# Attention over pairs 4 to 7 of a batch in one stretch instead of two

## The chip, the cores and the metric

The kernel runs on one core of a Trainium2 chip. The metric is the device time in microseconds; the kernel before takes 1127.67 us (median of three runs, 1126.29 to 1128.37). Work goes to TensorE (matrix products, from SBUF into the accumulators in PSUM), VectorE, ScalarE and GpSimd (elementwise work; the first two empty PSUM), and SyncE, whose queue issues DMAs. In a profile they are PE (PEld for its weight loads), DVE, ACT, POOL and SP.

## The reference

For x of shape (8, 512, 256), in float32, four blocks are added one after the other, each on a layer norm LN of x:

```python
# 1: linear attention       Q, K, V = n @ Wq.T, n @ Wk.T, n @ Wv.T      (n = LN(x))
x = x + l2norm(Q) * (sum over rows of l2norm(K) * V) / 512
# 2: gated feed-forward, p = LN(x) shifted down by one row
xr, xk = mu_r * n + (1 - mu_r) * p, mu_k * n + (1 - mu_k) * p
x = x + sigmoid(xr @ Wr.T) * (square(relu(xk @ Wk.T)) @ Wv2.T)
# 3: softmax attention, 16 heads of 64, with biases
x = x + concat(softmax(q k.T / 8, over the query axis) v) @ l_w.T + l_b
# 4: the same feed-forward as in 2, with the same weights
```

The softmax is over the query axis (axis 2 of the scores), so a key's row of scores holds its whole sum.

## The kernel before

Batches are processed as a pipeline. `linear`, `queries`, `mean`, `front`, `front_ffn` and `front_norm` (the "front") do blocks 1 and 2 and the norm of block 3 for a batch; each step that has to turn rows into columns goes through `normed_dma`: statistics on VectorE (L399, L400), a shift and a scale on GpSimd (L417 to L420), the normalisation on ScalarE (L423), a copy on GpSimd (L450), a transposing DMA on the SP queue (L455) and a copy on GpSimd (L459). For block 3 this leaves the tile `xta` (256 x 512, columns); `sums_of_rows` (L877) adds differences of its quarters, `xts`.

The 16 heads of a batch are eight pairs, p = 0 to 7; g = 8b + p numbers them over all batches. `project_pairs(g)` (L953) makes queries and keys of two pairs, g and g + 1, into two `qk` tiles, by a seven-product scheme for 2 x 2 blocks (`seven`, L898): seven products of TensorE, each of four matmuls with 256 columns (L968), and between them sums on VectorE and ScalarE (L920, L930, L940, L976, L984) on which later products depend. `values_fast` does the same for the values of four pairs (L1005), `project_out_fast` for the output (L1148), `keys` for one product of the last feed-forward (L623). The differences of weights and biases that the scheme needs are made at the start.

Attention of a pair is four steps c (128 keys of each head). `scores` (L1265) makes the scores of a step in eight matmuls on 64 x 64 quarters of the array (L1277), and VectorE takes their maxima (L1283); `exps` takes the exponentials on ScalarE with the sums beside (L1294); `scale_v` divides the values by the sums (VectorE L1307, GpSimd L1311); `context` (L1318) multiplies, again in eight quarter matmuls (L1331), and after the last step ScalarE and VectorE add the two halves (L1338, L1339). The context of a pair runs one pair or one step behind its scores.

Nothing is scheduled by the compiler: the program writes the instructions of every engine in the order that the class `Order` finds. It knows a modelled time for every step (`yield "V", 0.62, ready` is a step on VectorE of 0.62 us; T, A, G and S are TensorE, ScalarE, GpSimd and SyncE), keeps a modelled clock for each engine, and picks the step that can start first; `PLAN` gives each kind of step a due pair and a lead, and `CHOICES`, one entry for each window, shifts the window's share of TensorE time, the slack and the choice between steps. The main loop (L1400) goes over pairs by two: `attend(first)` is one stretch of attention for two pairs, in which other engines get steps only where `order.fill(0.0, 1.0)` finds them room; TensorE does nothing else there. Then comes a window of projections: `project_pairs` of the next two pairs is due in it, and front, values, output and last feed-forward (`tail`) of neighbouring batches fill it. So a batch has four stretches and four windows, behind pairs 1, 3, 5 and 7:

```python
    for first in range(0, G, 2):
        g = order.period = first + 1
        attend(first)
        if g + 1 < G:
            order.add(project_pairs(g + 1), "pairs", g)
        share = (total - order.spent) / ((G - first) // 2) + order.choice[0]
        order.until(g, share)
```

In the last batch the output is made plainly, in two halves (`project_out`), the first behind pair 5. The pool `heads` holds two `qk` tiles. Other things that the change touches: `vb` is the value bias, `dvb` the difference of its parts, `lb` the output bias, added to x by GpSimd in the last batch (L821); the squares for the norms of keys and queries go into a tile of their own, `sq` (L711, L742).

Of the kernel before, what the change touches and what calls it, by code (L numbers as in the profile page):

```python
# [8 lines left out]
F32 = mybir.dt.float32  # L9
U16 = mybir.dt.uint16  # L10
AF = mybir.ActivationFunctionType
ALU = mybir.AluOpType
# [18 lines left out]
PAIRS, BANKS = 3, 2  # L31
X_LANDS = (4.1, 8.5, 12.0)
# [7 lines left out]
    (0, 2, 3079, ((18, 1), (24, 1), (34, 1), (39, 2), (69, 1), (89, 1), (103, 1), (107, 1), (117, 1), (118, 1), (130, 1), (144, 1), (145, 1), (146, 1), (147, 2))),  # L40
    (0, 2, 24122, ((7, 3), (11, 1), (59, 1), (116, 2), (148, 1))),
    (-7, 1, 4847, ((5, 2), (8, 1), (13, 2), (15, 1), (24, 2), (25, 2))),
    (6, 0, 20556, ((24, 3),)), (3, -1, 86816, ((20, 1), (43, 1))),
    (4, 0, 84218, ((12, 1), (24, 2))), (-4, -1, 2976, ((40, 2),)), (0, 2, 77253, ((20, 1),)),
    (0, 2, 52854, ((34, 2),)), (6, 0, 62490, ((11, 3), (23, 1), (69, 2))),
    (-1, 0, 20876, ((7, 1),)), (-6, 0, 25653, ((58, 1),)), (-2, 1, 2103, ((72, 2),)),
    (-1, 0, 81629, ((7, 2), (8, 3), (67, 2))), (2, 0, 43246, ((52, 1),)),
    (0, 0, 79119, ((1, 2), (7, 1), (26, 2), (30, 2))), (6, -1, 2477, ()),
    (2, 0, 39734, ((33, 3),)),
    (-1, 1, 40203, ((14, 1), (31, 1), (32, 2), (38, 2), (55, 1), (60, 1))),  # L50
    (-1, 0, 0, ((1, 1), (20, 1), (25, 1), (37, 1))), (-2, 1, 35196, ((30, 1), (95, 2))),
    (-2, -1, 46703, ((16, 1), (66, 1))), (3, -1, 26797, ()),
    (-2, 2, 17874, ((9, 2), (10, 1), (20, 2))), (1, -1, 36974, ((2, 1), (7, 1))),
    (-2, 0, 3147, ((14, 3), (63, 1), (77, 3))),
    (4, 0, 77531, ((6, 2), (19, 2), (53, 3), (54, 1))), (-2, 2, 9675, ((18, 1), (42, 1))),
    (-1, 0, 83991, ((17, 2),)), (4, 2, 81239, ((31, 1),)), (-2, 2, 86574, ((24, 1),)),
    (-3, 0, 50919, ()), (0, -1, 4080, ()), (-2, 2, 82040, ((34, 1),)),
# [11 lines left out]
    "y rows": (4, 8), "y plain": (2, 0), "y last": (11, 16), "scale": (0, 128),  # L69
# [35 lines left out]
class Order:  # L105
# [5 lines left out]
    def __init__(self):  # L111
# [3 lines left out]
        self.last, self.asked = None, 0  # L115
# [101 lines left out]
    @property  # L217
    def choice(self):
        return CHOICES[min((self.period + 1) // 2, len(CHOICES) - 1)]
# [58 lines left out]
def kernel(ctx: ExitStack, tc: tile.TileContext, a: dict, out: bass.AP):  # L278
# [1065 lines left out]
    def attend(g):  # L1344

        for c in range(NT):
            if c == 3:
                order.at_once(scale_v(g, 0))
# [129 lines left out]
```

## Time and profile before

| | |
|---|---|
| median of three runs | 1127.67 us |
| the profiled execution | 1127.63 us, span 1125.9 us |
| stretches of attention | 32 of two pairs, 13.9 us each without waits (the first is cut in two) |
| windows of batch 2, behind pairs 1, 3, 5, 7 | 24.4, 16.6, 9.5, 31.2 us |
| other waits of TensorE | 6.2 us for the first normalised rows; 0.5 to 0.7 us at 44.7, 46.4 and 51.3 us |

The profile is of one execution. A window's or stretch's length is the time from its first matmul's start to the first start of what follows. Matmuls are pipelined and their ends are modelled, so lost time is read from starts. Engines other than TensorE cost time only where TensorE waits for them.

### The profile page before, as it was taken

The page shows a single profiled execution, that of the slowest core. Times are in us where ns is not written, and L with a number is a line of the kernel's source. Part 1 is how long each engine was busy: PE and PEld are TensorE (multiplying, and loading weights), DVE is VectorE, ACT ScalarE, POOL GpSimd, SP SyncE. Part 2 cuts the span into 40 slices and gives each one's busy share as a digit, 9 for nine tenths or more (in the row PEclk, how much of TensorE's full clock was granted, in tenths as well). Part 3 has the DMA queues.
Part 4 walks back from the last instruction along what each step waited for, and adds up shares of the span by engine and source line. Part 5 has one row for each costly group of instructions (what it writes and reads, how often), then busy time and mean ns, then how long its engine had stood idle before and what let it go on. Part 6 is the DMA issues. An engine that isn't in the chain of part 4 may idle for free. (4 is left out here: it accounts for less than half of the span.)

```text
span 1125.9 us, 19587 instructions
## 1 busy us (share of the span) xinstructions
PE 1107.2 (98%) x6938; PEld 699.6 (62%) x6938; DVE 801.4 (71%) x1743; ACT 677.2 (60%) x1779; POOL 589.1 (52%) x909
## 2 busy tenths in 40 slices
PE   7999999999999999999999999999999999999998
PEld 4655566665766657666567556676565764766556
DVE  5777677768676785777866777568786678666765
ACT  4666666468455774566745676447766377554653
POOL 4596346454465554654657456475454854344311
PEclk9999999999999999999999999999999999999999
DMA  8001001110112101111111211112100111001001
GB/s 302 11 10 30 10 2 20 20 29 10 20 38 39 29 10 29 34 34 20 21 29 47 20 29 20 42 24 29 26 20 23 29 29 21 1 20 29 19 1 38
DMA packets 83426, 34.18 MB, mean 30 GB/s; under 512 B 73088, under 2 KB 81920, under 8 KB 82816
## 3 DMA queue, kind: packets, MB, share of 16 engines
q1 hardware_dynamic: 82432, 31.87, 12.5%
q8 instruction: 55, 0.90, 0.3%
q10 hardware_dynamic: 864, 1.05, 0.3%
q14 instruction: 43, 0.35, 0.1%
q0 software_dynamic: 32, 0.00, 0.0%
HBM read 10.89 MB, written 4.19 MB: 13 GB/s over the span
## 5 line engine op out<-in xcount | busy, mean ns | idle before, releaser
L1294 ACT ACTIVATE e<-sc,nm 128x512 f32<-128x512 f32 x512 | 345.9, 690 | 113.4 <-DVE nm L1283 112.4
L1283 DVE TENSOR_REDUCE nm<-sc 128x1 f32<-128x512 f32 x512 | 322.6, 681 | 36.3 <-PE sc L1277 35.7
L1277 PE MATMUL sc<-qk 64*64 64x512 f32 x2048 | 267.1, 593 | 3.0 <-DVE qk L940 2.0
L1331 PE MATMUL cx<-e,vs 64*64 64x512 f32 x2048 | 264.8, 590 | 1.2 <-POOL vs L1311 1.2
L1311 POOL TENSOR_TENSOR vs<-v,rs 128x256 f32<-128x256 f32 x128 | 78.5, 615 | 261.5 <-DVE rs L1307 258.7
L1331 PEld LDWEIGHTS cx<-e,vs 64*64 64x64 f32 x2048 | 86.0, 133 | 136.1 <-issue 111.3
L1277 PEld LDWEIGHTS sc<-qk 64*64 64x64 f32 x2048 | 81.7, 133 | 133.7 <-issue 99.7
L1294 ACT ACTIVATION_READ_ACCUMULATOR e<-sc,nm 128x1 f32 x512 | 106.1, 207 | 0.0
L976 ACT ACTIVATE qk<-m_qk,bias 128x256 f32<-128x256 f32 x124 | 51.9, 472 | 51.8 <-PE m_qk L968 51.5
L1339 DVE TENSOR_TENSOR ctx<-cx,ctx 128x512 f32<-128x512 f32 x64 | 44.2, 691 | 41.2 <-ACT ctx L1338 40.8
L984 DVE SCALAR_TENSOR_TENSOR qk<-m_qk,dbias,qk 128x256 f32<-128x256 f32 x124 | 54.1, 478 | 22.4 <-PE m_qk L968 20.7
L1338 ACT COPY ctx<-cx 128x512 f32<-128x512 f32 x64 | 37.6, 587 | 38.3 <-PE cx L1331 38.0
L704 PE MATMUL kv<-wkv,xrFalse 128*128 128x512 f32 x112 | 54.0, 611 | 0.0
L459 POOL COPY xrFalse<-xkFalse 128x1024 uint16<-128x1024 uint16 x24 | 32.0, 1334 | 27.9 <-DMA xkFalse<-xrFalse 27.9
L450 POOL COPY xrFalse<-xnFalse 128x512 uint16<-128x512 uint16 x72 | 41.8, 613 | 6.2 <-ACT xnFalse L423 6.2
L1148 PE MATMUL m_y<-ctx,al 128*128 128x256 f32 x168 | 39.9, 381 | 0.0
L968 PE MATMUL m_qk<-xta,aq 128*128 128x256 f32 x124 | 39.0, 396 | 0.7 <-ACT qk L976 0.7
L968 PE MATMUL m_qk<-xta,sums_q 128*128 128x256 f32 x124 | 37.7, 385 | 0.0
L968 PE MATMUL m_qk<-xta,ak 128*128 128x256 f32 x124 | 36.9, 379 | 0.0
L968 PE MATMUL m_qk<-xts,ak 128*128 128x256 f32 x124 | 36.9, 379 | 0.0
L968 PE MATMUL m_qk<-xta,sums_k 128*128 128x256 f32 x124 | 36.9, 379 | 0.0
L968 PE MATMUL m_qk<-xts,aq 128*128 128x256 f32 x124 | 36.9, 379 | 0.0
(272 smaller groups left out, 2123.7 us busy)
## 6 DMA issues: line engine op xcount, KB each, us to landing
out<-x SPq DMA_DIRECT2D x16, 256.0 KB, 2.1
x<-in_x SPq DMA_DIRECT2D x6, 512.0 KB, 4.0
aq<-in_aq SPq DMA_DIRECT2D x1, 1024.0 KB, 8.4
ak<-in_ak SPq DMA_DIRECT2D x1, 1024.0 KB, 10.4
av<-in_av SPq DMA_DIRECT2D x1, 1024.0 KB, 12.4
al<-in_al SPq DMA_DIRECT2D x1, 1024.0 KB, 10.3
xkFalse<-xrFalse SPq DMA_TRANSPOSE x36, 3.1
x<-in_x SPq DMA_DIRECT2D x4, 128.0 KB, 3.6
```

Of the source, the lines that this page charges most:

```text
L450: nc.gpsimd.tensor_copy(apart.rearrange("p (l k u d) -> p l k u d", l=2, k=KC, u=2)[:, :, :, u, :], xn[:, u, :].rearrange("p (k d l) -> p ...
L704: nc.tensor.matmul(ps, lhsT=xt[:, kc, u * P : (u + 1) * P], rhs=wkv[:, kc, :], start=(kc == 0), stop=(kc == KC - 1),)
L968: nc.tensor.matmul(ps[:, w * HS : (w + 1) * HS], lhsT=lhs[w][n - 1], rhs=block_of_rows(b, n), start=start and w == 0, stop=True, skip_grou ...
L976: nc.scalar.activation(dst[:, w, :], ps[:, w, :], AF.Identity, bias=bias[:, w, p : p + 1])
L984: nc.vector.scalar_tensor_tensor(dst[:, w, :], ps[:, w, :], dbias[:, w, p // 2 : p // 2 + 1], part[:, w, :], ALU.add, ALU.add,)
L1148: nc.tensor.matmul(ps, lhsT=lhs[n - 1][:, g, :], rhs=rhs[g][n - 1], start=first and g == 0, stop=True, skip_group_check=True,)
L1277: nc.tensor.matmul(ps[j][m * HD : (m + 1) * HD, :], lhsT=kt[hs, keys], rhs=qt[hs, :], start=True, stop=True,)
L1283: nc.vector.tensor_reduce(nm[:, j : j + 1], ps[j], AX.X, ALU.max, negate=True)
L1294: nc.scalar.activation(e[:, j, :], ps[j], AF.Exp, bias=nm[:, j : j + 1], accum_out=sums[g, h][:, c % 2, j : j + 1],)
L1311: nc.gpsimd.tensor_tensor(vs, vh[b, p // 4][:, 2 * h : 2 * h + 2, cols].rearrange("p t (j d) -> p t j d", j=2), rs.unsqueeze(3).to_broadca ...
L1331: nc.tensor.matmul(cx[m][j * HD : (j + 1) * HD, :], lhsT=vsc[g, c // 2][ks, c % 2, j, :], rhs=es[g, c][ks, j, :], start=(c == 0), stop=(c ...
L1339: nc.vector.tensor_tensor(ct, cx[1], ct, ALU.add)
```

## The change

A batch now has three stretches, of pairs 0 and 1, 2 and 3, and 4 to 7, and three windows, behind pairs 1, 3 and 7. The window behind pair 3 has two `project_pairs`, for pairs 4/5 and 6/7, and the pool of `qk` tiles has four. A window's share of TensorE's time goes by the number of pairs in the stretch before it. `CHOICES` has a new list, one entry for the start and one for each of the 24 windows.

The room in SBUF for two more `qk` tiles comes from elsewhere: `sq` goes (the squares are written where the product, or the queries, are written afterwards); the tile `sums` is made for one of two buffer sets; `lb` goes, and its 256 numbers are loaded late in batch 6's output into a block of weight sums that is no longer used, from where GpSimd adds them in batch 7; `vb` keeps half of its numbers, and `dvb` holds the other half until the first plain values are made (two additions of 256 columns instead of one of 512), and only then becomes the difference. The first output half of batch 7 comes behind pair 7, since there is no window behind pair 5.

```diff
-    heads = ctx.enter_context(tc.tile_pool(name="heads", bufs=2))
+    heads = ctx.enter_context(tc.tile_pool(name="heads", bufs=4))
...
-    vb = const.tile([P, H * HD], F32, tag="vb", name="vb")
-    lb = const.tile([P, 1, D], F32, tag="lb", name="lb")
+    vb = const.tile([P, 2, 2 * P], F32, tag="vb", name="vb")
...
-    nc.sync.dma_start(out=vb, in_=a["vb"].partition_broadcast(P))
+    for half in range(2):
+        for dst, at in ((vb, 0), (dvb, 1)):
+            cols = slice((2 * half + at) * 2 * P, (2 * half + at + 1) * 2 * P)
+            nc.sync.dma_start(out=dst[:, half, :], in_=a["vb"][cols].partition_broadcast(P))
...
-    nc.sync.dma_start(out=lb[:, 0, :], in_=a["lb"].partition_broadcast(P))
...
-            sq = one.tile([P, D], F32, tag="sq", name=f"sqk_{b}_{h}_{u}")
-            nc.scalar.activation(sq, ps[:, :D], AF.Square, accum_out=ss[:, u : u + 1])
+            nc.scalar.activation(
+                kv[:, u, :], ps[:, :D], AF.Square, accum_out=ss[:, u : u + 1]
+            )
...
         if b == B - 1:
-            yield "G", 1.3, ready
-            xh = xb[:, 2 * h : 2 * h + 2, :]
-            nc.gpsimd.tensor_tensor(xh, xh, lb.to_broadcast([P, 2, D]), ALU.add)
+            order.add(biased(b, h, ready), "bias", NP * b)
+
+    def biased(b, h, ready):
+
+        yield "G", 1.3, ready, -1, "lb"
+        xh, lb = x[b][:, 2 * h : 2 * h + 2, :], blocks["sums_y"][:, 0:1, :D]
+        nc.gpsimd.tensor_tensor(xh, xh, lb.to_broadcast([P, 2, D]), ALU.add)
...
-            nc.vector.tensor_tensor(vh[b, half][:, t, :], ps, vb[:, cols], ALU.add)
+            for i, part in enumerate((vb, dvb)):
+                at = slice(i * 256, i * 256 + 256)
+                nc.vector.tensor_tensor(
+                    vh[b, half][:, t, at], ps[:, at], part[:, half, :], ALU.add
+                )
             order.give()
         order.marks[f"v_{b}_{half}"] = ready
+        yield "G", 1.3, ready
+        nc.gpsimd.tensor_tensor(dvb, dvb, vb, ALU.subtract)
+        order.marks["dvb"] = ready
...
+            nc.sync.dma_start(
+                out=blocks["sums_y"][:, 0, :D], in_=a["lb"].partition_broadcast(P)
+            )
+            order.marks["lb"] = p4 + 2.5
...
-    def attend(g):
...
+    def attend(first, n):
+
+        for g in range(first, first + n):
+            behind = 1 if g > first else 0
+            for c in range(NT):
+                if c == 3 and g < first + n - 1:
+                    order.at_once(scale_v(g, 0))
+                scores(g, c)
+                if c == 1 and g > first:
+                    order.at_once(scale_v(g - 1, 1))
+                if g > 0 and c >= behind:
+                    context(g - 1, c - behind)
+                elif g == 0:
+                    order.fill(BANK)
+                if behind and c == 3:
+                    context(g - 1, 3)
+                exps(g, c)
+                order.fill(0.0, 1.0)
...
-    halves_of = vb.rearrange("p (g i c) -> p g i c", i=2, c=2 * P)
-    nc.gpsimd.tensor_tensor(dvb, halves_of[:, :, 1, :], halves_of[:, :, 0, :], ALU.subtract)
...
-    for first in range(0, G, 2):
-        g = order.period = first + 1
+    lengths = {NP * b + 4: 4 for b in range(B)}
+    first = 0
+    while first < G:
+        n = lengths.get(first, 2)
+        g = order.period = first + n - 1
+        order.step += 1
...
-        if p == 5 and b == B - 1:
+        if p == 3 and b == B - 1:
             order.add(project_out(b, 0), "y plain", g)
...
-        if g + 1 < G:
-            order.add(project_pairs(g + 1), "pairs", g)
+        for i in range(1, lengths.get(g + 1, 2), 2):
+            if g + i < G:
+                order.add(project_pairs(g + i), "pairs", g)
...
-        share = (total - order.spent) / ((G - first) // 2) + order.choice[0]
+        share = (total - order.spent) * n / (G - first) + order.choice[0]
```

## The prediction

> **What bounds the kernel now.** I read the page's busy shares first, then TensorE's timeline around the places where it changes between attention and projections, then the eight windows behind pair 5 of each batch, and last VectorE's timeline at a late start of attention. The page, engine shares and granted clock:
>
> ```profile
> PE 1107.2 (98%) x6938; PEld 699.6 (62%) x6938; DVE 801.4 (71%) x1743; ACT 677.2 (60%) x1779; POOL 589.1 (52%) x909
> ...
> PEclk9999999999999999999999999999999999999999
> ```
>
> TensorE is the bound nearly everywhere, at its full clock. The change takes no matmul away, so only TensorE time that is no streaming can go. Two such kinds show. The first is the price of changing the tiling; TensorE's timeline at an undisturbed start of attention (stretch of pairs 6 and 7, batch 3), then at an end (batch 2). Columns are start, length up to the modelled end, engine, line:
>
> ```profile
> 541.24 1.89 PE L471 MATMUL r_g<-fr,xrTrue 128*128 128x256 f32 x8
> 543.06 1.09 PE L1277 MATMUL sc<-qk 64*64 64x512 f32 x8
> 543.97 1.04 PE L1331 MATMUL cx<-e,vs 64*64 64x512 f32 x8
> 544.83 1.04 PE L1277 MATMUL sc<-qk 64*64 64x512 f32 x8
> ```
>
> ```profile
> 414.81 1.07 PE L1277 MATMUL sc<-qk 64*64 64x512 f32 x8
> 415.67 1.93 PE L1331 MATMUL cx<-e,vs 64*64 64x512 f32 x16
> 417.52 1.13 PE L1005 MATMUL m_v<-av,xta 128*128 128x256 f32 x4
> 418.49 0.59 PE L968 MATMUL m_qk<-xta,aq 128*128 128x256 f32 x2
> ```
>
> Read starts, not lengths. Inside a stretch a block of eight matmuls starts 0.858 us after the one before (median of the rows), and a 128x256 projection matmul takes 0.2155 us start to start. Going in, the r_g matmuls need 1.82 us, not 8 x 0.2155 = 1.72 (0.09 lost), and the first block 0.91, not 0.86 (0.05). Going out, the last block takes about 0.11 too long and the first four m_v 0.97, not 0.86 (0.10). One break of attention costs 0.36 us, and the other undisturbed stretches show the same gaps.
>
> The second kind is waits. The windows behind pair 5, batch 0 to 7 (stretch, its length, busy times of the engines):
>
> ```profile
> 137.71:148.97 11.26, 10.19 (x46) 7.89 (x43) 6.91 (x16) 5.77 (x17) 4.71 (x8) 1.00 0.00 0
> 257.81:266.30 8.49, 8.49 (x40) 6.46 (x36) 6.85 (x19) 6.12 (x15) 4.40 (x9) 1.00 0.03 6
> 394.12:403.63 9.51, 8.51 (x41) 6.63 (x37) 7.92 (x23) 7.55 (x18) 5.86 (x11) 1.00 0.14 27
> 532.21:543.06 10.85, 10.17 (x47) 8.04 (x45) 8.94 (x25) 8.36 (x20) 7.33 (x13) 1.00 0.26 50
> 670.83:680.83 10.00, 10.00 (x49) 8.06 (x45) 8.49 (x25) 6.71 (x16) 6.48 (x12) 1.00 0.17 15
> 807.07:815.55 8.48, 8.48 (x40) 6.45 (x36) 6.85 (x19) 6.11 (x15) 4.40 (x9) 1.00 0.03 6
> 943.42:951.81 8.39, 8.39 (x41) 6.54 (x37) 6.75 (x19) 7.21 (x17) 5.07 (x11) 1.00 0.16 31
> 1060.82:1072.46 11.64, 11.64 (x56) 9.73 (x52) 8.04 (x21) 7.43 (x18) 3.67 (x5) 1.00 0.12 23
> ```
>
> They hold 28 matmuls of the pairs 6 and 7 (6.0 us) and little else: 8 to 24 others, so 7.8 to 11.2 us of streaming. Length less streaming is 1.34, 0.71, 1.73, 1.34, 0.50, 0.71, 0.61 and 0.41 us, together 7.35. Of each, 0.18 is the tiling (the windows behind pairs 1, 3 and 7 with no wait all show 0.18), so waits hold 7.35 - 8 x 0.18 = 5.9 us. They come from the chain of seven products, which waits for ScalarE and VectorE between its steps; here nothing else is there to run.
>
> A third kind sits inside stretches: after a late start VectorE drags its reductions along. Batch 4, start at 656.52, VectorE, then the TensorE row it ends in:
>
> ```profile
> 656.71 0.69 DVE L601 SCALAR_TENSOR_TENSOR xkFalse<-xkFalse,o_f 128x512 f32<-128x512 f32 x1 [0.15 <-PE o_f L471]
> 657.86 0.48 DVE L494 TENSOR_SCALAR prev_g<-edge_g,omu 128x1 f32<-128x1 f32 x2 [0.46 <-ACT prev_g L549]
> 658.43 0.87 DVE L555 SCALAR_TENSOR_TENSOR xkTrue<-xrTrue,mu,prev_g 128x256 f32<-128x256 f32 x2
> 659.22 3.67 DVE L1283 TENSOR_REDUCE nm<-sc 128x1 f32<-128x512 f32 x6
> ```
>
> ```profile
> 665.52 1.09 PE L1331 MATMUL cx<-e,vs 64*64 64x512 f32 x8 [0.18 <-POOL vs L1311]
> ```
>
> Such stretches lost 0.80 (batch 3, pair 4), 0.41 (batch 4, pair 4), 0.92 and 0.08 us (batches 6 and 5, pair 6), by their length over 16 x 0.858 us.
>
> **The change, part by part.** The sum goes against the profiled execution: span 1125.9 us, 1127.63 with what lies around it, 0.04 below the median of the runs, 1127.67.
>
> Eight breaks fewer: 8 x 0.36 = -2.9 us. No rival undoes this unless a stretch breaks elsewhere.
>
> The windows behind pair 5 go, and their streaming joins other windows. Behind pair 3 the chains of pairs 4/5 and 6/7 run side by side, beside k_f, r_f and o_f, 16.4 us of streaming now. The ten windows behind pairs 1 and 3 of batches 1 to 5, 16.6 and 24.4 us long, hold waits of at most 0.03 us, though they hold the same chains: -5.9 us, bounded by 0 (all waits come back) and -5.9. I take the whole, since the new windows are like these. The window behind pair 3 of batch 7 is bare too: 28 matmuls, 6.05 us, in 7.66; 1.43 are waits. With two chains it should lose as little as the better short ones (0.2): -1.2, between 0 and -1.4.
>
> The new windows behind pair 3 end with more VectorE work (a second chain's sums, 0.69 and 0.88 each), so late starts get likelier. If each batch pays the mean of the four late ones, 0.55 us, it is +4.4; what goes is 0.80 + 0.41 + 0.92 + 0.08 = 2.2: +2.2, between -2.2 (none) and 8 x 0.92 - 2.2 = +5.2.
>
> Inside the long stretch a pair repeats the one before: VectorE's reductions end as late behind their scores in the second pair (2.38 us for the last) as in the first, ScalarE's exponentials restart in the same phase, and TensorE waits for nothing in the second pair of undisturbed stretches. Per pair VectorE needs 2 x 1.29 + 2.47 for the reductions, 0.69 and 2 x 0.17 = 6.1 of 6.87 us: 0.8 us a pair remain. Nothing accumulates: 0. The scaled values reach TensorE 0.4 us ahead (row of L1311 against L1331) at each change of pair, five a batch now, four before: 0, while GpSimd stays free there.
>
> The start: the subtraction for dvb on GpSimd (1.27 us for this shape) moves from ahead of the work to behind values(0, 0), into a GpSimd queue busy from 60 to 97 us; between 0 and +1.3, I take +0.5. The value adds split from 0.69 us into two of about 0.4, +0.5 us on VectorE, hidden as TensorE waits there for ScalarE (L799). SP issues three loads more and lb's less: 3 x 0.44 - 0.65 = +0.7 us of its queue ahead of al and x, and al is first used at 94 us: 0. The lb load late in the kernel waits on SP for TensorE's product 5, ahead of the rows' transposes; the al load before it already waits there for product 7: 0, at most its issue (0.65). The squares written into kv and r add no instruction; VectorE's product waits already for that square (L712): 0. Four query/key buffers only take away waits: 0. The lb addition (2.5 us, GpSimd) moves from batch 6 into batch 7, where GpSimd is under half busy: 0. The first half of batch 7's output (6.9 us) moves behind pair 7, ahead of the last contexts, where 3.5 us sufficed to cover the last exponentials: 0.
>
> Sum: -2.9 - 5.9 - 1.2 + 2.2 + 0.5 = -7.3 us; 1120.3 us. All bounds together: -2.9 - 5.9 - 1.4 - 2.2 = -12.4 (1115.2) on the good side, -2.9 + 5.2 + 1.3 = +3.6 (1131.2) on the bad.
>
> **Rivals.** *Only the breaks are gained.* The waits move to the starts of the long stretches, or to the ends of the windows behind pair 3, because two chains end there together. 1127.6 - 2.9 = 1124.7. For it: the short windows' last wait is VectorE's closing sum (L940), which stays. Against: ten clean windows.
>
> *Slower: the front's norm misses its window.* In a stretch VectorE and ScalarE hardly run anything else; in batch 3 the second half's statistics (L399) run at 533.44, in the window that goes, though o_f ended at 517.6. If they wait for the window behind pair 7, the next batch's queries and values wait for statistics 1.13, L417 to L420 1.54, L423 1.08, L450 1.17, transpose 3.1, L459 1.33, rows 4 x 0.73: 12.3 us. Cover: 14 matmuls of keys, 16 of r_g, 16 of o_g, 9.9 us. 2.4 us open in each of 7 batches, 1120.3 + 17 = 1137; from 1.0 us a batch on, the change is no gain. Against: the window behind pair 3 grows by 6.0 us to about 523.6, and from 517.6 on the chain through L423 needs 0.7 + 1.3 + 1.1 + 1.5 + 1.1 = 5.7 us. It just fits.
>
> *Same:* waits of 0.5 to 1.2 us a batch, by a smaller miss of this kind: 1125.4 to 1129.9.
>
> *The stretch drifts.* If the work of the window that goes (statistics 2 x 1.13, mixes 0.48 + 3 x 0.87: 5.4 us) were placed inside, beside the 2.9 us of other VectorE work in the two stretches now (batch 2), it would pass the 4 x 0.8 us free by 5.1 us: far slower, 1120.3 + 7 x 5.1 = 1156. The trace has such work only at the starts and ends of stretches. [...]
>
> **How the numbers follow.** Forecast (1117 to 1122.5): 0.54; better than 1117: 0.03; only the breaks (1122.5 to 1125.4): 0.17; same: 0.10; norm misses: 0.12; drift: 0.04. 0.2% is 2.3 us, about what a measurement of this kernel can tell. Faster 0.74, same 0.10, slower 0.16. Leaving out no more than 0.2 takes the range to 1117 to 1130; the forecast's own is 1117 to 1122.5.
>
> **What would show it.** 24 blocks of attention, eight of them near 27.5 us; windows behind pair 3 of 22 to 25 us with 0.2 us over their streaming; late reductions at the long stretches' starts, under 1 us each. Wrong: TensorE waiting behind pair 7 for xta or xts (L459, L877), or waits in the third or fourth pair of a stretch.

## The result, and the profile after

The changed kernel takes 1124.42 us (median, 1123.14 to 1125.14), the kernel before 1127.26 in the same comparison: a ratio of 0.9973, with a 95% interval of 0.9964 to 0.9983. It is faster, by 2.8 us where 7.3 were forecast, and lies outside the forecast's 1117 to 1122.5. The profiled execution has a span of 1122.6 us against 1125.9, so 3.2 to 3.3 us have to be found in it.

The page of the changed kernel, busy shares and granted clock:

```profile
PE 1106.4 (99%) x6938; PEld 742.7 (66%) x6938; DVE 799.6 (71%) x1747; ACT 678.6 (60%) x1779; POOL 589.9 (53%) x909
...
PEclk9999999999999999999999999999999999999999
```

The bound is as before: TensorE, at full clock (1.000 over the span), with as many matmuls. So the difference must lie again in breaks and waits, and the reading is again by start-to-start times: 0.858 us for a block of attention, 0.2155 us for a projection matmul; what a window or a stretch takes beyond that is its excess, of which 0.18 us is the tiling.

The new windows behind pair 7, batches 1, 3 and 6 (stretch, its length, busy times of the engines):

```profile
276.85:310.01 33.16, 33.16 (x138) 25.61 (x136) 20.64 (x47) 17.04 (x47) 18.15 (x30) 1.00 0.13 23
...
550.59:583.79 33.20, 33.20 (x138) 25.67 (x137) 19.92 (x48) 17.27 (x47) 17.99 (x31) 1.00 0.09 17
...
956.87:985.92 29.05, 26.77 (x120) 21.74 (x119) 16.27 (x35) 11.16 (x24) 15.66 (x21) 1.00 0.10 28
```

In batches 1 to 5 these windows stream 32.78 us; in batch 6 25.49, and TensorE is busy for only 26.77 of 29.05. In the rows, r, k and o are the feed-forward's products with Wr, Wk and Wv2, f stands for the first feed-forward (block 2) and g for the last (block 4). The TensorE timeline of batch 6:

```profile
956.87 1.99 PE L473 MATMUL r_f<-fr,xrFalse 128*128 128x256 f32 x8
958.70 1.89 PE L473 MATMUL o_f<-fv,xnFalse 128*128 128x256 f32 x8
961.60 3.72 PE L473 MATMUL r_g<-fr,xrTrue 128*128 128x256 f32 x16 [1.01 <-DVE xrTrue L557]
...
969.97 3.72 PE L473 MATMUL o_g<-fv,xnTrue 128*128 128x256 f32 x16 [1.28 <-ACT xnTrue L643]
973.53 1.03 PE L1014 MATMUL m_v<-av,xta 128*128 128x256 f32 x4
974.47 0.70 PE L977 MATMUL m_qk<-xta,aq 128*128 128x256 f32 x2
```

Half of r_f and o_f stands behind the long stretch. In the kernel before both halves of batch 6 were done behind pair 3, the second one here (TensorE's timeline; the next stretch starts at 929.53):

```profile
925.98 1.89 PE L471 MATMUL r_f<-fr,xrFalse 128*128 128x256 f32 x8
927.71 1.89 PE L471 MATMUL o_f<-fv,xnFalse 128*128 128x256 f32 x8
```

Now the chain of pairs 6 and 7 has that place, and the window behind pair 7 begins with steps that wait for each other: in the rows of the changed kernel above, r_g for the mix (the step xr = mu_r n + (1 - mu_r) p), o_g for the keys' activation. The values and the chain of queries and keys (m_v, m_qk), which could have run beside, come after them. Excess 3.56 us, so 3.4 us of waits.

The second thing to see is VectorE at the start of a long stretch, here batch 2, whose first scores start at 385.47:

```profile
385.69 0.69 DVE L949 TENSOR_TENSOR qk<-m_qk,qk 128x512 f32<-128x512 f32 x1
386.30 0.47 DVE L496 TENSOR_SCALAR prev_g<-edge_g,omu 128x1 f32<-128x1 f32 x2
386.86 0.87 DVE L557 SCALAR_TENSOR_TENSOR xkTrue<-xrTrue,mu,prev_g 128x256 f32<-128x256 f32 x2
387.74 0.06 DVE L493 MEMSET prev_g<- 128x2 f32 x1
387.89 0.87 DVE L557 SCALAR_TENSOR_TENSOR xkTrue<-xrTrue,mu,prev_g 128x256 f32<-128x256 f32 x2
388.68 3.67 DVE L1303 TENSOR_REDUCE nm<-sc 128x1 f32<-128x512 f32 x6
```

Two key mixes (xk) of the last feed-forward stand ahead of the first maxima, which start 3.2 us behind the scores. This stretch has 0.72 us of waits.

The account of the span, before to after:

| place | us |
|---|---|
| eight breaks fewer | -2.9 |
| waits behind pair 5, gone | -5.9 |
| batch 7, window behind pair 3, 1.43 to 0.11 | -1.3 |
| waits inside stretches, 3.5 to 5.4 | +1.9 |
| waits behind pair 7, 0.15 to 4.8 (3.4 in batch 6, 0.2 to 0.6 in batches 1 to 4) | +4.7 |
| waits behind pairs 1 and 3 | +0.4 |
| startup and end | -0.1 |

These add to -3.2. Inside the stretches of the changed kernel nearly all of it are late starts: six in long stretches with 0.3 to 0.7 us each (3.6) and some in short ones with 1.75 together. In the kernel before, 1.3 of the 3.5 us were something else, which the prediction's list of late starts leaves out. In batch 4's stretch of pairs 2 and 3, which starts in time, a context waited for GpSimd's scaling of the values, and that stood behind four other steps of GpSimd:

```profile
634.61 1.09 PE L1331 MATMUL cx<-e,vs 64*64 64x512 f32 x8 [1.07 <-POOL vs L1311]
```

So the late starts alone rose by some 3.1 us, from 2.2, and this one wait went.

### The profile page after: what moved, and what is told of

It reads as the page before. It is cut to its first block, busy times and chain, and to the rows that moved or that the text cites. A ratio compares the mean times of both kernels' runs of the same rounds, so it can differ in the third digit from the quotient of the medians.

```text
span 1122.6 us, 19674 instructions
## 1 busy us (share of the span) xinstructions
PE 1106.4 (99%) x6938; PEld 742.7 (66%) x6938; DVE 799.6 (71%) x1747; ACT 678.6 (60%) x1779; POOL 589.9 (53%) x909
## 4 chain that ended last, share of the span: by engine, by line
PE 96%; DVE 2%; ACT 1%; POOL 1%; issue 0%; DMA 0%; DVEq 0%; ACTq 0%
PE sc L1297 20%; PE cx L1351 20%; PE m_qk L977 17%; PE m_v L1014 8%; PE m_y L1164 8%; PE kv L706 5%; PE o_g L473 3%; PE r_g L473 2%; PE q L473 2%; PE k_f L585 2%; PE r_f L473 2%; PE m_k_g L625 2%; PE o_f L473 2%; PE y L473 1%; PE v L1053 1%; PE qk L1269 1%
## 5 line engine op out<-in xcount | busy, mean ns | idle before, releaser
L1297 PE MATMUL sc<-qk 64*64 64x512 f32 x2048 | 283.0, 593 | 0.1
L1351 PE MATMUL cx<-e,vs 64*64 64x512 f32 x2048 | 282.1, 590 | 0.0
L1351 PEld LDWEIGHTS cx<-e,vs 64*64 64x64 f32 x2048 | 107.0, 133 | 116.4 <-issue 78.1
L1297 PEld LDWEIGHTS sc<-qk 64*64 64x64 f32 x2048 | 105.5, 132 | 112.2 <-issue 65.7
```

Source lines behind the costliest of these rows:

```text
L1297: nc.tensor.matmul(ps[j][m * HD : (m + 1) * HD, :], lhsT=kt[hs, keys], rhs=qt[hs, :], start=True, stop=True,)
L1351: nc.tensor.matmul(cx[m][j * HD : (j + 1) * HD, :], lhsT=vsc[g, c // 2][ks, c % 2, j, :], rhs=es[g, c][ks, j, :], start=(c == 0), stop=(c ...
```

## Experiments

All times are medians, with the ratio to the kernel before on the same chip; "0.18" is again the excess that the tiling makes by itself. The startup differs between profiled executions (the first of the mixes starts at 61.1 us in the changed kernel, at 60.2 in the run with the mixes behind the reductions), so places are compared, not only spans.

### What a break costs

```diff
+        if g % NP == 6 and c == 0:
+            nc.tensor.matmul(
+                ps[0][:, :HS], lhsT=aq[:, 0, :P], rhs=ak[:, 0, :HS], start=True, stop=True
+            )
```

> Adds one product of 128x128 by 128x256 (two matmul rows, 0.43 us of streaming) between pairs 5 and 6 in each of the eight long stretches, into a PSUM bank that the scores overwrite; nothing else moves. Theory A (a break of attention costs 0.36 us beyond its streaming): each long stretch grows by 0.43 + 0.36 = 0.79 us, the whole by 6.3 us, to 1130.7 us. Theory B (the gaps at a break belong to the projections' chains and not to the change of tiling): each grows by 0.43 us, the whole by 3.4 us, to 1127.9 us.

1130.34 us, ratio 1.0029 [1.0017, 1.0041]: 5.9 us above the changed kernel. Its TensorE timeline at such a place:

```profile
261.95 2.20 PE L1355 MATMUL cx<-e,vs 64*64 64x512 f32 x16
264.08 0.70 PE L1294 MATMUL sc<-ak,aq 128*128 128x256 f32 x2
264.71 1.95 PE L1301 MATMUL sc<-qk 64*64 64x512 f32 x16
```

Two full-array matmuls stream 0.43 us and take 0.63 from start to start; the other 0.16 us of a break are in the two halves of the stretch. Eight times 0.36 and 0.43 is 6.3, and 5.9 is measured. Theory A: the term of the breaks is right.

### The side parts alone

```diff
-    heads = ctx.enter_context(tc.tile_pool(name="heads", bufs=2))
+    heads = ctx.enter_context(tc.tile_pool(name="heads", bufs=3))
...
-            sq = one.tile([P, D], F32, tag="sq", name=f"sqk_{b}_{h}_{u}")
-            nc.scalar.activation(sq, ps[:, :D], AF.Square, accum_out=ss[:, u : u + 1])
+            nc.scalar.activation(
+                kv[:, u, :], ps[:, :D], AF.Square, accum_out=ss[:, u : u + 1]
+            )
```

> The kernel before, with its own order and windows, and three of the change's side parts alone: the squares of the key and query norms written in place of into a tile of their own, one sums tile in place of two, three query/key buffers in place of two. Theory A (these cost and give nothing on the path): 1126.8 to 1127.8, ratio 1.000. Theory B (the two tiles' freeing or the third buffer takes a wait of the windows behind pair 5 away, so that part of the gain was to be had without the new order): 1122 to 1125.

1126.41 us, ratio 0.9992 [0.9983, 1.0001]. The interval holds no change; if there is a gain, it is at most 2 us and most likely half a microsecond. So the gain is most likely the new order's. The moves of vb, dvb and lb and the fourth buffer are not in this run.

### The late starts: what they cost and by what law

The first run leaves the mixes out.

```diff
+                if name[0] == "g" and i == 1:
+                    out_cols, in_cols = dst[:, kc, :], xr[:, kc, :]
...
+            mixes = not (name[0] == "g" and i == 1)
+            if mixes:
+                first_column(ps, name, h, i)
-            for kc in range(KC):
+            for kc in range(KC if mixes else 0):
```

> Leaves out part of the computation: the multiply-add with mu_k and the first column of the key input in the last feed-forward of batches 0 to 6 (VectorE, L496 and L557 into xkTrue, 2.3 us a long stretch), ScalarE writes the scaled rows there instead; the order is the same. Theory A (a long stretch loses how late its first reductions run beyond 3.77 us, counted from the first scores): the six long stretches that lose 0.34 to 0.73 us now start their reductions before 3.77 us and lose less than 0.05 us each: -3.6 us, to 1120.8 us. Theory B (VectorE's and ScalarE's own work drifts over four pairs): the losses stay at 0.3 us or more a stretch, and the time within 1.2 us of the changed kernel's.

1120.44 us, ratio 0.9943 [0.9928, 0.9959]. Every long stretch now has an excess of 0.18: theory A. So the mixes at the starts cost 3.6 us in the changed kernel, by the stretches, and 4.0 by the time.

The second run makes starts later that were in time.

```diff
+        if g % NP == 0 and g > 0 and c == 0:
+            late = small.tile([P, 2], F32, tag="st", name=f"late_{g}")
+            for j in range(2):
+                nc.vector.tensor_reduce(late[:, j : j + 1], aq[:, j, :S], AX.X, ALU.max)
```

> The changed kernel with two more VectorE reductions (of a weight tile, 128x128 each, into a small tile nobody reads) ahead of the first reductions of pair 0 in batches 1 to 7: they cost about 1.4 us on VectorE at the start of each of those stretches. There the second reduction's start comes after the first scores' start by 2.43, 3.13, 3.59, 4.16, 3.13, 3.13 and 2.43 us in batches 1 to 7. Theory A (a stretch loses what its first reductions come later than 3.77 us, and nothing below): losses of about 0, 0.7, 1.2, 1.75, 0.7, 0.7, 0 in place of 0, 0, 0, 0.38, 0, 0, 0, in all 4.7 us more, 1129. Theory B (the stretch takes a late start up again in its later pairs, since VectorE has slack there): 1124.4 to 1126. Theory C (VectorE is the bound of the stretch, each microsecond counts): 7 starts by 1.4, some 9.5 us, 1134.

1127.71 us, ratio 1.0005 [0.9996, 1.0014], 3.3 us above the changed kernel. The expectation calls the listed times the start of the second reduction; they are its ends. They were to come 1.36 us later and came 1.18 later in batches 2 to 6: an added reduction lasts 0.68 us, but the next one starts 0.60 us after it. In batches 1 and 7 they came 0.75 later, since VectorE had been idle there. With the measured ends the law holds to 0.02 us:

| batch | end of the second reduction, us behind the first scores | minus 3.77 | waits measured |
|---|---|---|---|
| 1 and 7 | 3.18 | below 0 | 0.00 |
| 2, 5 and 6 | 4.31 | 0.54 | 0.53 |
| 3 | 4.78 | 1.01 | 1.00 |
| 4 | 5.34 | 1.57 | 1.55 |

A stretch loses exactly what its first maxima come later than 3.77 us, once, and nothing accumulates. Theories B and C fall. The ten late starts of the changed kernel, in long and short stretches, follow the same law to 0.02 us.

### The waits behind pair 7

The first attempt changes the share of batch 6's window behind pair 3, so that both halves of r_f and o_f fit.

```diff
-    (1, 0, 8349, ((31, 2), (71, 2)))
+    (6, 0, 8349, ((31, 2), (71, 2)))
```

> Only one number of the order's table is changed: the share of the window behind pair 3 of batch 6, 1 to 6, so that the feed-forward of the second half (r_f, o_f: 16 matmuls, 3.4 us) is issued before the long stretch and not behind it. Theory A (the 3.4 us that the changed kernel waits in the window behind pair 7 of batch 6 come from that late half: its norm is the next batch's input): that window's loss falls from 3.56 us to under 1 us, a loss of up to 1 us may appear behind pair 3, and the time falls by 2 to 3.4 us, to 1121.0 to 1122.4 us. Theory B (waits that are taken away in one window come up in another, the sum of them stays): the time stays within 1 us of the changed kernel's.

1127.21 us, ratio 1.0 [0.9992, 1.0009]. The window behind pair 7 fell from 3.56 us of excess to 2.10 and the long stretch to 0.18, but the window behind pair 3 rose to 4.90. Its end on TensorE:

```profile
930.05 0.59 PE L977 MATMUL m_qk<-xta,sums_k 128*128 128x256 f32 x2
933.53 1.22 PE L977 MATMUL m_qk<-xts,aq 128*128 128x256 f32 x2 [2.88 <-DVE qk L993]
934.54 1.06 PE L977 MATMUL m_qk<-xts,ak 128*128 128x256 f32 x2
935.39 1.06 PE L977 MATMUL m_qk<-xta,sums_q 128*128 128x256 f32 x2
```

The second chain was left alone there, and waited for a sum that stood on VectorE behind statistics and mixes. After the wait two matmuls took 0.76 to 1.01 us instead of 0.43. Neither theory gave this time. The run is confounded and settles nothing about batch 6 beyond that the waits can move.

The second attempt keeps rows between the chain's products.

```diff
-    (1, 0, 8349, ((31, 2), (71, 2)))
+    (6, -1, 8349, ((1, 2), (2, 1), (2, 3), (8, 3), (24, 1), (31, 2), (34, 1), ...))
```

> The changed kernel with another entry 20 of CHOICES alone: share 6 in place of 1 and another order of the steps of batch 6's window behind pair 3, so that all eight products of r_f and o_f stand ahead of the long stretch and the window behind pair 7 begins with the second chain and the values, not with rows that wait for each other. The first run of this question left the second chain bare at the window's end and was confounded; here the rows stand between the chain's products. Theory A (the 3.4 us of wait in batch 6's window behind pair 7 come from two steps issued behind the long stretch): that window keeps at most 1.5 us of wait, mostly for the last rows (o_g behind the keys' activation), the window behind pair 3 at most 0.6, and the time falls by 2 to 3 us from 1124.4 to 1121.4 to 1122.4. Theory B (the last batches have too little independent work left, wherever the steps stand): waits of 3 us or more stay in the two windows together, 1124 to 1125.

1123.97 us, ratio 0.9973 [0.9963, 0.9983]: the changed kernel's time within the measurement. The window behind pair 7 lost 1.6 of its 3.4 us of waits; o_g still waits for the keys' activation, since nothing is left to run beside it:

```profile
981.75 3.50 PE L473 MATMUL o_g<-fv,xnTrue 128*128 128x256 f32 x15 [1.11 <-ACT xnTrue L643]
```

What the window gave back, the long stretch ahead of it took (excess 0.52 to 1.60), with 0.4 more behind pair 3: the rows' statistics and mixes now stand on VectorE at the stretch's start. For batch 6, theory A and theory B are each half right.

The third run makes the same misplacement in a batch where it did not exist: batch 4, whose window behind pair 7 had 0.63 us of waits.

```diff
-    (-4, 0, 38293, ((53, 3),))
+    (-8, 0, 38293, ((53, 3),))
```

> The changed kernel with the share of batch 4's window behind pair 3 at -8 in place of -4 and nothing else: one step less fits, so the second half of o_f is issued behind the long stretch, and the window behind pair 7 begins with rows that wait for each other, as batch 6's does. Theory A (the miss alone makes the wait, in any batch): batch 4's window behind pair 7 waits 2.5 to 4 us where it waited 0.6, and the time is 1126.5 to 1128. Theory B (in a middle batch the next batch's front, queries and differences fill the place): under 1 us of wait there, 1124.2 to 1125.2.

1129.57 us, ratio 1.002 [1.0011, 1.0029]: 5.2 us above the changed kernel, more than either theory said. TensorE behind pair 7 of batch 4:

```profile
685.48 1.99 PE L473 MATMUL o_f<-fv,xnFalse 128*128 128x256 f32 x8
688.97 3.69 PE L473 MATMUL r_g<-fr,xrTrue 128*128 128x256 f32 x16 [1.49 <-DVE xrTrue L557]
...
693.96 1.13 PE L625 MATMUL m_k_g<-sums,sums_f 128*128 128x256 f32 x4 [0.87 <-POOL sums L618]
...
699.01 3.72 PE L473 MATMUL o_g<-fv,xnTrue 128*128 128x256 f32 x16 [1.84 <-ACT xnTrue L643]
```

One step, 1.7 us of streaming, issued behind the long stretch brings this window to 5.76 us of excess and the next stretch, by a late start, to 0.86. It is theory A with a larger price: the order that `Order` then finds puts r_g, the keys and o_g first, each behind a chain of VectorE, GpSimd and ScalarE, and the values and the queries' chain, which wait for nothing, behind them. So bunched steps make the waits behind pair 7 in both batches where they stood at the window's head. The 0.2 to 0.6 us of batches 1 to 4 stand at single steps further back, and their cause was not tried.

### Is it the order or the structure?

Entries 1 to 24 of `CHOICES` were searched for the least modelled time, with windows and stretches as in the change:

> The changed kernel with another table of choices for its 24 windows (the entry for the start stays), found by a search over the order's own modelled times; there the waits outside the start and the stretches' ends nearly go, -18.7 us in the model. Theory A (what the change lost of the forecast lies in the order, in late halves and late starts): the time falls by 4 to 8 us, to 1116 to 1120 us, with under 3 us of waits in the windows behind the first and under 3 us in the stretches. Theory B (the chains set the waits, whatever the order): it stays above 1122 us.

1127.61 us, ratio 1.0008 [0.9999, 1.0017]: theory B by the number, but for another reason. The search had found a hole in the model: products of the output projection that add onto a bank count as ready at once, while on the chip they waited for the step that reads the bank, 1.95 us here. TensorE in the window behind pair 1 of batch 3:

```profile
477.53 1.89 PE L1171 MATMUL m_y<-ctx,sums_y 128*128 128x256 f32 x8
481.36 3.58 PE L1171 MATMUL m_y<-ctx,sums_y 128*128 128x256 f32 x8 [1.95 <-DVE xnTrue L1184]
```

Another 2.9 us went in one stretch of batch 7, where the output bias, which the change loads late, came too late: GpSimd waited for it, and the scaling of the values stood behind the steps that followed.

```profile
1030.07 1.28 POOL L835 TENSOR_TENSOR x<-x,sums_y 128x512 f32<-128x512 f32 x1 [4.49 <-DMA sums_y<-in_lb]
...
1035.83 1.09 PE L1358 MATMUL cx<-e,vs 64*64 64x512 f32 x8 [2.71 <-POOL vs L1338]
```

With the hole closed and entries 2 to 22 searched anew, the mixes staying where the planner has them:

```diff
-        def product(n, mark, ps=None):
-            ready = yield "T", 2 * FAST, 0.0, -1, mark, ps is None
+        def product(n, mark, ps=None, since=0.0):
+            ready = yield "T", 2 * FAST, since, -1, mark, ps is None
...
-        _, _, p2 = yield from product(2, None, ps1)
+        _, _, p2 = yield from product(2, None, ps1, u1)
```

> The searched order of the run with the putting-off of both mixes (1130), with the mixes where the planner has them, in PSUM and ahead of the first reductions. Nothing is left out. In the run with the putting-off the windows waited 13.6 us in all, startup included, against 17.5 in the changed kernel, and batch 6's window behind pair 7 had no wait left. Theory A (the waits behind pair 7 belong to the order written out, not to the structure; the late starts stay): 1119.5 to 1122. Theory B (waits leave the windows and come back at the starts of the stretches): 1122.5 to 1126.

1121.23 us, ratio 0.9949 [0.9936, 0.9962], 3.2 us below the changed kernel. Startup left out, the excess of all windows fell from 11.0 to 7.8 us, and batch 6's behind pair 7 is at 0.18; the stretches stayed where they were together (10.8 to 11.2). Theory A. The same stretch of batch 7 lost 1.8 us in this order, again from GpSimd's queue and the late bias:

```profile
1023.82 1.27 POOL L835 TENSOR_TENSOR x<-x,sums_y 128x512 f32<-128x512 f32 x1 [4.19 <-DMA sums_y<-in_lb]
...
1027.66 1.33 POOL L1239 COPY xnTrue<-xkTrue 128x1024 uint16<-128x1024 uint16 x1
1028.92 0.61 POOL L1338 TENSOR_TENSOR vs<-v,rs 128x256 f32<-128x256 f32 x1
...
1029.59 1.09 PE L1358 MATMUL cx<-e,vs 64*64 64x512 f32 x8 [1.55 <-POOL vs L1338]
```

### Are the late starts a matter of place?

The mixes stand ahead of the maxima because `take_pair` runs every step that holds a score bank before the first scores are issued. In these runs ScalarE writes the shifted half into the mix's destination, and the mix is issued later; the order on TensorE, GpSimd and SyncE stays.

```diff
+            put_off = i == 1 and name[0] in ("g",)
+            if put_off:
+                order.take()
+                ps = dst
...
+            behind_scores(put_off, mix_of, ps, name, h, i, dst, xr)
...
+                if g == first and c:
+                    issue_put_offs(1 if c < 3 else 99)
```

> The changed kernel with its order of steps on TensorE, ScalarE's steps, GpSimd and SyncE as it is; only the key mixes of the last FFN that stand at the start of an attention stretch are issued behind the second and the third reductions of the stretch's first pair instead of ahead of the first ones (ScalarE writes the shifted half into the mix's destination instead of into a PSUM bank, so that the scores need not wait for the bank). Nothing is left out. Theory A (the late starts of the long stretches come from these mixes' place alone, and VectorE has the room for them two score blocks later): the long stretches of batches 1 to 6 fall from 0.52 to 0.90 us of wait to about 0.2 each, the time by some 3.5 us from 1124.4 to 1120.4 to 1121.4, as with the mix left out (1120.4). Theory B (the lateness only moves to the later reductions): the stretches lose as much at their fourth scores, 1123.5 to 1125. Theory C (the keys' chain on GpSimd starts later and its products wait behind pair 7): the stretches gain 3.5 and the windows behind pair 7 give back 1 us or more, 1121.5 to 1124.

1127.46 us, ratio 1.0004 [0.9995, 1.0013]: 3 us worse than the changed kernel, and worse than any theory said. The long stretches of batches 1 to 4 have 1.8 to 2.0 us of excess. VectorE and GpSimd in the long stretch of batch 1:

```profile
251.88 0.73 POOL L910 TENSOR_TENSOR xts<-xta 128x256 f32<-128x256 f32 x1
251.96 1.79 DVE L552 SCALAR_TENSOR_TENSOR xkTrue<-xrTrue,mu,xkTrue 128x256 f32<-128x256 f32 x2
252.68 0.79 POOL L910 TENSOR_TENSOR xta<-xta 128x256 f32<-128x256 f32 x1
253.55 0.79 POOL L910 TENSOR_TENSOR xts<-xta 128x256 f32<-128x256 f32 x1
...
255.17 0.88 DVE L552 SCALAR_TENSOR_TENSOR xkTrue<-xrTrue,mu,xkTrue 128x256 f32<-128x256 f32 x2
```

The mix now reads both tensors from SBUF, and beside GpSimd's differences it takes 1.79 us, alone 0.88. That and the second mix one block later were too much for VectorE. In batch 6, where GpSimd ran beside the mixes for only 0.1 us, they took 0.88 us and the stretch's excess fell to 0.18. The same with both kinds of mixes put off, in batch 6's other order and in the searched one, gave 1131.25 and 1129.96:

> The same putting-off, also for the key mixes of the first FFN (late at the starts of pair 2), together with the other entry 20 of CHOICES for batch 6 (share 6, both halves of r_f and o_f ahead of the long stretch), which alone gave 1124.0. Nothing is left out. Theory A (the three are separate losses): the long stretch of batch 6 loses its 1.4 us, the starts of pair 2 in batches 2, 3 and 6 fall by about 1 us together, 1118.5 to 1120.3. Theory B (with the order of batch 6 the lost time only moves between its two windows and its stretch, and the short stretches' lateness has other causes): 1120.3 to 1121.5.

> The same putting-off of both key mixes, in an order of entries 2 to 22 that was searched again with the planner told one thing more: the products of the output projection that add onto a bank wait for the step that reads what stands there (its being left out let the earlier searched order lose what it gained). Windows keep their number and their sizes. Theory A (most of what the change lost sits in the order, and this order has no bunched rows behind pair 7): waits behind pair 7 under 0.5 us each, batch 6 too, stretches at 0.2 to 0.4: 1114 to 1118. Theory B (the planner still leaves something out, and the waits come up behind pair 1 or at starts): 1119 to 1125.

Ratios 1.0032 [1.0021, 1.0042] and 1.0024 [1.0015, 1.0033], above every theory's range. In the searched order without the putting-off (above) the same windows gave 1121, so putting off both kinds cost 8.7 us there. These three runs speak against this place, not against another one. The next puts the mixes into the second pair, where GpSimd is through.

```diff
+                if (g - first, c) in ((1, 1), (1, 3), (2, 0), (2, 2), (3, 0), (3, 2)):
+                    issue_put_offs(1)
```

> The changed kernel with its own order; the key mixes of the last FFN that stand at the start of the long stretches are issued in the stretch's second pair, one behind the second and one behind the fourth block of scores. ScalarE writes the shifted half into the mix's destination, as before in the run that put them only one and two blocks off, where the first of them took 1.5 to 1.9 us (0.9 alone) beside GpSimd's differences of the same time. Nothing is left out. Theory A (late starts are a matter of place alone: VectorE has the room once its start is on time and GpSimd is through): the long stretches of batches 1 to 6 wait about 0.2 us each, the time falls by 3 to 3.7 us from 1124.4 to 1120.7 to 1121.4. Theory B (VectorE has no room anywhere in the stretch: 0.9 us put in anywhere comes out as a wait): 1124 to 1126. Theory C (the mixes slow beside GpSimd there as well): long stretches at 0.4 to 1 us, 1122 to 1125.

1124.65 us, ratio 0.9974 [0.9964, 0.9984], the changed kernel's time. The starts were in time in all six, and a new wait of 0.54 to 0.64 us stood in their place, always at the same block. In batch 1:

```profile
259.34 0.88 DVE L553 SCALAR_TENSOR_TENSOR xkTrue<-xrTrue,mu,xkTrue 128x256 f32<-128x256 f32 x2
260.13 0.17 DVE L1354 RECIPROCAL rs<-sums 128x4 f32<-128x4 f32 x1
260.38 0.61 POOL L1358 TENSOR_TENSOR vs<-v,rs 128x256 f32<-128x256 f32 x1 [4.20 <-DVE rs L1354]
...
261.05 1.52 PE L1378 MATMUL cx<-e,vs 64*64 64x512 f32 x12 [0.36 <-POOL vs L1358]
```

The reciprocal stood behind the mix, the scaling behind the reciprocal, the context behind the scaling. The second mix, behind a fourth block, had cost nothing, which speaks against theory B, though the number is B's. So both go there:

```diff
-                if (g - first, c) in ((1, 1), (1, 3), (2, 0), (2, 2), (3, 0), (3, 2)):
+                if (g - first, c) in ((1, 3), (2, 3), (3, 1), (3, 2), (3, 3)):
```

> The changed kernel with its own order; the key mixes of the last FFN that stand at the start of the long stretches are issued one behind the fourth block of scores of the second pair, one behind that of the third, where VectorE stood idle before the context's sum and no reciprocal follows. Nothing is left out. Theory A (place alone): the long stretches of batches 1 to 6 wait 0.2 us each in place of 0.5 to 0.9, the time falls by 3 to 3.7 us from 1124.4 to 1120.7 to 1121.4. Theory B (VectorE has room for it nowhere): 0.3 us or more a stretch remain, 1122.5 to 1125.

1120.54 us, ratio 0.994 [0.9927, 0.9954]: as much as with the mixes left out, with nothing left out. VectorE in the long stretch of batch 2, whose first scores are at 384.22:

```profile
384.45 0.69 DVE L976 TENSOR_TENSOR qk<-m_qk,qk 128x512 f32<-128x512 f32 x1
385.36 1.29 DVE L1330 TENSOR_REDUCE nm<-sc 128x1 f32<-128x512 f32 x2 [0.22 <-PE sc L1324]
...
397.97 0.88 DVE L553 SCALAR_TENSOR_TENSOR xkTrue<-xrTrue,mu,xkTrue 128x256 f32<-128x256 f32 x2
398.84 0.69 DVE L1386 TENSOR_TENSOR ctx<-cx,ctx 128x512 f32<-128x512 f32 x1
```

All long stretches are at 0.18. It is place alone. Before that, in the searched order, the mixes had been put into the second pair too, where they met the reciprocal again, and batch 6's window behind pair 3 rose to 1.50 us of excess:

> The searched order with the key mixes of the last FFN put off to the second pair of the long stretches as well. Nothing is left out. Theory A (both losses are of order and place, and add up): 3 to 3.7 us below the searched order alone, 1116 to 1118.5. Theory B (one of them does not hold in this order): within 1 us of the searched order alone.

1124.71 us, ratio 0.998 [0.9971, 0.9989], 3.5 us above the searched order alone, which neither theory gave. With the mixes at the pairs' ends and batch 7's entry as in the change:

> The searched order (1121.2) with entry 22, batch 7's window behind pair 1, as in the changed kernel, and with the key mixes at the ends of the second and third pairs of the long stretches. Nothing is left out. Theory A (late starts and waits are separate, and the 1.8 us of batch 7 belong to entry 22): 1.8 and some 2.5 us less, 1116.5 to 1118.5. Theory B (entry 22 is not the cause, or the order ahead of the stretches needs the mixes where they are): 1119 to 1122.

1119.78 us, ratio 0.9932 [0.992, 0.9945]: the best of all, 4.6 us below the changed kernel and 7.7 below the one before. It is less than the sum of its parts: by the number it is theory B. Batch 7's stretch is back at 0.17, so entry 22 was its cause. But batch 6's window behind pair 3 is at 1.50 again, and the long stretches of batches 6 and 4 kept 1.2 and 0.9 us of waits. In batch 6 mixes still stand ahead of the first maxima, whose second one ends 1.2 us behind the 3.77 of the law; in batch 4 the context waits for GpSimd's scaling, behind GpSimd's differences of xta:

```profile
666.23 1.09 PE L1385 MATMUL cx<-e,vs 64*64 64x512 f32 x8 [0.70 <-POOL vs L1365]
```

No run tried to take these waits away.

## Why the prediction was wrong in size

*Eight breaks, -2.9:* right. The added breaks cost 0.35 us each by the trace (28.41 us of a long stretch in place of 27.63, less 0.43 of streaming); by the time, 5.9 us for all where 6.3 were expected.

*Waits behind pair 5, -5.9 taken whole:* this is the step that failed. The windows and their waits did go, and behind pairs 1 and 3 only 0.4 us came back, as the prediction argued from the ten clean windows. But it looked at those windows only. The chain that a vanished window had carried takes room in another one, and what stood there has to move: in batch 6 a half of r_f and of o_f went behind the long stretch, to the head of the window behind pair 7. In the windows behind pair 7 4.7 us of waits came back, 3.4 of them in that one place: the term is -0.8, not -5.9. The run in batch 4 shows that such a miss makes the waits, 5.2 us for one step, and the searched order that it is no matter of the structure: with as many windows, batch 6's behind pair 7 is free of waits there. Why 1.3 us came back in batches 1 to 4 stays open.

*Batch 7, -1.2:* right, -1.3.

*Late starts, +2.2:* right in kind; that the size fits (+1.9) is partly luck. The forecast had 4.4 us of them, one in each batch. The long stretches pay 3.6 and the short ones, which it did not count, 1.75. Against these stand the 2.2 us of its list and the 1.3 us of the wait for GpSimd in batch 4, which it did not list either. What the prediction did not see is that this loss could be had back, 3.6 us of it by place.

*Inside the stretch, 0:* right. The third and fourth pairs of a long stretch repeat the second, and the law of the late start shows a loss taken once. The rival of the drift falls: clean stretches of four pairs run at 0.858 us a block to the end (27.63 us in batches 0 and 7 of the changed kernel, 0.18 of it the tiling). Where VectorE got two mixes more close together, in the run with the mixes behind the reductions, TensorE waited for it, for two to three blocks: the long stretches of batches 1 to 4 had 1.8 to 2.0 us of excess.

*The start, +0.5 and zeros:* startup excess was within its own scatter (0.9 us between the changed kernel and the run with the mixes behind the reductions), and the three side parts that were tried alone gave no measurable change. The late load of lb, put at 0, cost nothing in the changed kernel; in two of the searched orders GpSimd waited 4.5 and 4.2 us for it, and a stretch lost 2.9 and 1.8 us.

*The rivals.* "Only the breaks are gained" names 1124.7 and came closest, by number; its mechanism (waits at the starts and behind pair 3) did not happen, the late starts of the long stretches (3.6) were no more than forecast (4.4), and the gain of 1.3 in batch 7 is not in it. "The front's norm misses its window" had the right place, behind pair 7, and the right cause, work that lost its window coming too late; it had the chain wrong (the norm's transpose, where it was the feed-forward's mix, sums and activation) and the extent (seven batches, where it was one). Its price of 2.4 us a batch was low: 3.4 and, forced in batch 4, 5.2. It should have been weighed batch by batch: towards the end the window behind pair 3 is shorter (22.6 us in batches 1 to 4, 20.9 in batch 5, 19.4 in batch 6), and there it no longer "just fits".

## What to carry to other kernels

When a window of work is taken away, its waits go, but so does its room: list each step that it carried, find the place where that step will stand instead, batch by batch, and ask what will wait behind it. On an engine that is not the bound, the place of a microsecond decided here, not the amount: the same 1.7 us of VectorE work (two mixes) cost 0.3 to 0.7 us ahead of a stretch's first reductions, 1.6 to 1.8 next to GpSimd's differences, 0.5 to 0.6 with one mix of the two ahead of a reciprocal, and nothing behind a pair's last block. And a search by a model ends in whatever dependency the model leaves out, so look for the new waits before believing the order.

## What was not expected of the hardware

A VectorE operation with two tensors in SBUF slowed beside GpSimd. The mix of 128x256 took 0.48 us with one operand in PSUM, in every one of 28 places of the changed kernel (473 to 482 ns), also beside copies on GpSimd. With both operands in SBUF, in the run with the mixes behind the reductions, two in a row took 0.88 us where GpSimd was idle (0.87 in the changed kernel), 1.48 to 1.80 beside its differences, and 1.94 in batch 4, where the first of them ran beside a copy; the longest single one took 1.07. The runs show the slowing, not its cause.

After two of the waits inside a kernel TensorE ran at about half rate. In the run with batch 6's share changed, 2.9 us of wait were followed by 3.5 us of matmuls at about 0.43 us instead of 0.2155; the view by stretches has the granted clock there in the third column from the right:

```profile
933.53:937.00 3.47, 3.47 (x8) 2.52 (x8) 2.50 (x6) 1.52 (x4) 3.06 (x5) 0.54 0.26 53
```

The first searched order shows the same after 1.95 us of wait (0.59 over the 4.1 us behind it). In these two, some eight matmuls cost 0.2 us more each, 1.7 us on top of the wait itself. The length of the wait alone does not decide it: in the run on batch 4 waits of 1.5 and 1.8 us left the clock at 1.00, and behind the 2.71 us in batch 7 of the first searched order eight quarter matmuls took 1.09 us, as at an undisturbed start of attention. What does decide was not tried.
